# Rotary embedding of the context: from GpSimd to VectorE, in place, in a four-layer decoder kernel

## The chip, the cores and the metric

The kernel runs on one core of a Trainium2 chip. The metric is the time of one execution on the device, in microseconds; before the change the median of three runs is 2383.44 us (2382.97 to 2384.99). The engines are named as in the profile: PE (TensorE, matrix products), DVE (VectorE), ACT (ScalarE), POOL (GpSimd) and SP (SyncE, which here only issues DMA transfers). Each engine works through its own instructions in order and waits for the others by semaphores.

## The reference, cut to what matters

Sixteen sequences of 56 tokens, 256 wide, pass through four layers. Each has an attention on a context of 1500 rows of 64 numbers per sequence and a feed-forward part. Layer 0 attends to the first 56 context rows only (the causal mask leaves no more), and its feed-forward part routes each token to 4 of 16 experts and adds two shared experts. Layers 1 to 3 attend to the whole context, rotated by position:

```python
# layer 0
x = x + jnp.tanh(g_xattn[0]) * _L0_xattn_ref(_layernorm(x), ctx_512, ...)
x = x + jnp.tanh(g_ffn[0]) * _L0_ffn_ref(_layernorm(x), ...)      # 16 experts, top 4, 2 shared
# layer 1 (2 and 3 use the same rotated context)
kv_rope = kv_c * cos[None] + _rotate_half(kv_c) * sin[None]
k_r     = jnp.einsum('bld,hdr->bhlr', kv_rope, W_kr)
scores  = jnp.einsum('bhsr,bhlr->bhsl', q_r, k_r)
ctx_c   = jnp.einsum('bhsl,bld->bhsd', jax.nn.softmax(scores), kv_rope)
```

`_rotate_half(x)` is the second half of the 64 numbers with its sign turned, followed by the first half; the kernel's sine table carries that sign.

## The kernel before, in words

Two sequences make a tile of 112 tokens, so there are 8 tiles (NT). The rotated context of all sequences lies in one buffer, `kv`: 125 partitions, and in each, for each tile, 12 rows of 2 sequences of 64 numbers. It stays in SBUF for the whole kernel. Layer 1 reads it first (L688), when layer 0 is done.

**Layer 0's attention** (`attention_mha`, L380 on) is a pipeline over the 8 tiles (loop at L597): in step i, PE makes the scores of tile i (L509, L515), the transposes of tile i-1 (L540) and its values (L549), and the projection of tile i-2 (L570); DVE takes maxima and differences (L529, L530), ACT the exponentials (L533), and DVE adds the result to the tokens (L573). From step 4 on, the router works through the tiles in four batches of two (`token_tiles`, L1024): DVE normalises the tokens (L1034, L1035; the inverse root by iteration, L131 to L141; L1040), PE transposes (L1048) and multiplies (L1056), DVE takes a softmax and ranks the experts (L1059 to L1074), PE counts places (L1091, L1093), DVE makes the list of slots (L1097 to L1102), and POOL scatters the tokens to their slots in `rows` in DRAM, eight indirect DMAs a batch (L1106). `rows` has been filled with zeros by 16 transfers from SP (`clear_rows`, L1162). All instructions stand in program order on their engines (`in_order`), so a router instruction that waits holds back the attention behind it on DVE and on PE.

**The rotation** (`Roping`, L863) is done on POOL. The context of a tile is loaded to a staging buffer `raw` (two of them, L874) by SP; POOL multiplies it with the cosines into `kv` (L880) and then, for each half, multiplies the other half with the sines (L885) and adds (L886): five instructions a tile. Tiles 0 to 3 are rotated in steps 0 to 3 of the attention; a load waits until POOL has released its staging buffer. Tiles 4 to 7 are rotated during the routed tiles, one part at every second tile; the loads of tiles 6 and 7 are issued just before that loop.

**The routed tiles** (`moe`, L1165; `tiles`, L1283): when the router is done, `table` (L1117) turns the counts into a list of tiles of 128 rows, of which the profiled execution has 34 in layer 0. SP reads the list and loads, three tiles ahead, a tile's expert weights (`wgu` L1197, `wd` L1198) and rows (`xrow` L1204). In tile i, PE multiplies with gate and up weights (L1223), transposes the hidden values of tile i-1 (L1234) and the rows of tile i+1 (L1211), and multiplies tile i-2 with the down weights (L1245); ACT applies the activation (L1227), DVE multiplies (L1228), copies the transposed hidden values (L1236) and makes the list of destinations (L1215); POOL scatters the results (L1248). `during` (L1304) is called at the end of each tile: it places the rotation's parts and, at every fourth tile, a part of the shared experts (L1414, L1425, L1426, L1431, L1433), and from tile 23 on POOL's diagonal matrices (L1318).

Of the kernel before, what the change touches and what calls it, by code (L numbers as in the profile page):

```python
# [36 lines left out]
F32 = mybir.dt.float32  # L37
# [4 lines left out]
ALU = mybir.AluOpType  # L42
# [3 lines left out]
B, S, D = 16, 56, 256  # L46
L, DC = 1500, 64
H = 16
TP = 2 * S
NT = B // 2  # L50
KP, KC = 125, 12
# [14 lines left out]
def bcast(ap, axis, n):  # L66

    ap = ap.unsqueeze(axis)
    shape = list(ap.shape)
    shape[axis] = n  # L70
    return ap.to_broadcast(shape)
# [3 lines left out]
def flamingo_kernel(ctx: ExitStack, tc: tile.TileContext, d: dict, out: bass.AP):  # L75
    nc = tc.nc
# [9 lines left out]
    in_order = tc.keep_in_program_order  # L86
# [20 lines left out]
    kv = const.tile([KP, NT, KC, 2, DC], F32, name="kv")  # L107
# [272 lines left out]
    def attention_mha(router, roping):  # L380
        with ExitStack() as st:
# [10 lines left out]
            def load(name, shape, src, queue):  # L392
                w = ap1.tile(shape, F32, name=name)
                in_order(queue.dma_start(w, src))
                return w


            k0 = ap1.tile([TP, NT, DC], F32, name="k0")

            def load_k0(b, queue):  # L400
                in_order(queue.dma_start(k0[S * b : S * b + S], d["ctx"][:, 0:S, :].rearrange("(t b) s c -> b s t c", b=2)[b]))

            load_x(0, nc.sync)
            load_k0(0, nc.scalar)
# [23 lines left out]
                    in_order(nc.gpsimd.tensor_copy(vbs[i][:, b, :, 32:34], bcast(small[0:TP, C_M : C_M + 2], 1, H // 2)))  # L428
            router.load_weights()
            wo = load("wo", [128, 2, D], d["L0_wo"], nc.gpsimd)  # L430
            for t in range(2):
                roping.load(t, nc.sync)
            clear = clear_rows(ap1)
            for _ in range(6):
                next(clear)
# [2 lines left out]
            for half in range(2):  # L438
# [3 lines left out]
                o = k0d[:, 8 * half : 8 * half + 8]  # L442
                i = bcast(ps[0:DC, 0 : 4 * TP].rearrange("p (n s) -> p n s", s=S), 2, 2)
# [153 lines left out]
            for i in range(NT + 2):  # L597
                new, turn, last = at(i), at(i - 1), at(i - 2)
                if turn:
                    turn.turned()  # L600
                if last:
                    last.turn_context()
                route(i, "a")
                if new:
                    new.scores()
                route(i, "b")
                route(i, "c")
                if new:
                    new.shift()
                    new.exps()  # L610
                route(i, "b")
                if turn:
                    turn.values()
                if last:
                    last.project()
                if turn:
                    turn.normalize()
                if last:
                    last.add()
                if i == 0:  # L620
                    turn_normed(1)
                    queries(1)
                if i + 1 < NT:
                    keys(i + 1)
                    pairs[i + 1].vb = make_values(i + 1)
                route(i, "c")
                route(i, "a")
                route(i, "b")
                route(i, "a")
                route(i, "b")  # L630
                if i < 4:
                    roping.rope(i)
                    roping.load(i + 2, nc.sync)
                    for _ in range(5):
                        next(clear, None)
                if i == 4:
                    load_absorbed(1, 0)
                    load_absorbed(1, 1)
# [223 lines left out]

    class Roping:  # L863
        def __init__(self, pool):
            self.pool, self.raw = pool, {}
            self.cos = pool.tile([KP, KC, DC], F32, name="cos")
            self.sin = pool.tile([KP, KC, DC], F32, name="sin")

        def load(self, t, queue, pool=None):
            if t == 0:  # L870
                in_order(queue.dma_start(self.cos, d["cos_k"]))
                in_order(queue.dma_start(self.sin, d["sin_k"]))
            self.raw[t] = (pool or self.pool).tile([KP, 2, KC, DC], F32, name="raw", bufs=2)
            in_order(queue.dma_start(self.raw[t], d["ctx"][2 * t : 2 * t + 2].rearrange("b (p c) e -> p b c e", c=KC)))  # L874

        def parts(self, t):
            hd = DC // 2
            raw = self.raw.pop(t)
            o = kv[:, t].rearrange("p c b e -> p b c e")
            in_order(nc.gpsimd.tensor_tensor(o, raw, bcast(self.cos, 1, 2), ALU.mult))  # L880
            yield
            for h in range(2):
                mine, other = slice(h * hd, (h + 1) * hd), slice((1 - h) * hd, (2 - h) * hd)
                rot = self.pool.tile([KP, 2, KC, hd], F32, name="rot")
                in_order(nc.gpsimd.tensor_tensor(rot, raw[:, :, :, other], bcast(self.sin[:, :, mine], 1, 2), ALU.mult))  # L885
                in_order(nc.gpsimd.tensor_tensor(o[:, :, :, mine], o[:, :, :, mine], rot, ALU.add))  # L886
                yield

        def rope(self, t):
            for _ in self.parts(t):  # L890
                pass

        def rest(self, st):

            late = st.enter_context(tc.tile_pool(name="rope2", bufs=1, reuse_waits="tile"))
            for t in range(6, NT):
                self.load(t, nc.sync, late)
            for t in range(4, NT):
                yield from self.parts(t)


    class Router:
# [254 lines left out]
    def clear_rows(pool):  # L1157

        zero = pool.tile([128, DX], F32, name="zero")
        in_order(nc.gpsimd.memset(zero, 0.0))  # L1160
        for e in range(16):
            in_order(nc.sync.dma_start(rows[e * CT : (e + 1) * CT].rearrange("c p x -> p c x"), bcast(zero, 1, CT)))  # L1162
            yield

    def moe(r, nxt=None, tail=None, rest=None):  # L1165
# [5 lines left out]
        with ExitStack() as st:  # L1171
# [85 lines left out]
            if l == 0:  # L1257


                sh = Shared(pool, ps_h, ps_o, side)  # L1260
                now = [part for e in range(2) for part in sh.parts(e, 0)]
                between = [part for e in range(2) for part in sh.parts(e, 1)]
                before, last = tail
                next(last)
                now[0][0]()
                next(before)
                next(last)
                next(last)
                next(before)
                next(last)  # L1270
                next(last)
                now[1][0]()
                next(last)
                r.table()
                next(last)
                next(last)
                next(last)
            else:
                r.table()
# [24 lines left out]
            def during(i):  # L1304
                if l == 2 and i == 3:
                    load_absorbed(3, 2)
                if i % 2 == 0 and rest:
                    next(rest, None)
                if i % 4 == 3 and between:
                    for work in between.pop(0):  # L1310
                        work()

                every, ahead = (1, n_sure - 4 - i) if l == 0 else (2, n_sure - 3 - i)
                if ahead >= 0 and ahead % every == 0 and ahead // every < len(by_pe):
                    t = by_pe[len(by_pe) - 1 - ahead // every]
                    diag[t] = pd.tile([TP, top, TP], F32, name=f"diag{t}")
                    for j in range(top):
                        in_order(nc.gpsimd.tensor_scalar(diag[t][:, j, :], ident[0:TP, 0:TP], r.weight[:, t, j : j + 1], None, ALU.mult))  # L1318

            weights, loads = [], []  # L1320
            if l == 0:
                weights = [load_weights(i) for i in range(3)]
                for part in now[0:2]:
                    part[1]()
                for part in now[2:]:
                    for work in part:
                        work()
                r.temporary.close()
                loads = [load_rows(i) for i in range(3)]
                rest = rest(st)  # L1330
                next(rest)
                pd = pool("d", 1)
                r.finish_weights()
            else:
                pd = pool("d", 1)
                r.finish_weights()
                occupy(14 if l == 3 else 8)
                if l == 2:
                    nxt.absorb(0)
# [207 lines left out]
    with tc.tile_pool(name="rope", bufs=1) as rope, routed(0) as r:  # L1547
        roping = Roping(rope)
        tail = attention_mha(r, roping)
        nxt = Next(1)  # L1550
        moe(r, nxt, tail, roping.rest)
    with ExitStack() as keep:
        f1w = keep.enter_context(tc.tile_pool(name="f1w", bufs=1, reuse_waits="tile"))
        matrix = f1w.tile([128, 2, D], F32, name="w8"), f1w.tile([128, 4], F32, name="sc")
# [3 lines left out]
        nxt = Next(2)  # L1558
# [7 lines left out]
    with routed(2) as r:  # L1566
        attention_mla(2, nxt, r)
        nxt.whole.close()
        nxt = Next(3)
# [71 lines left out]
def _arrange(i):  # L1641
    a = {
        "x": i["x"].reshape(B * S, D),
        "ctx": i["ctx_512"],
        "g_xattn": i["g_xattn"].reshape(1, 4),
        "g_ffn": i["g_ffn"].reshape(1, 4),
    }
# [9 lines left out]
    for l in (1, 2, 3):  # L1657
        p = f"L{l}_xattn_"
# [61 lines left out]
```

## Time and profile before

| what | value |
|---|---|
| median of three runs | 2383.44 us |
| profiled execution, its own time | 2402.98 us |
| its span | 2401.2 us |
| granted PE clock, mean | 0.963 |
| layer 0's attention: last addition to the tokens (L573) | 140.65 us |
| first and last routed tile of layer 0 (L1223) | 184.67 and 308.77 us |
| POOL's rotation: 8 L880, 16 L885, 16 L886 | 27.9, 29.5, 29.5 us |
| context loads L874 | 8 of 750 KB |

Times in the table's lower part are from the span's start. The profile gives each engine's busy time and, for the time that an engine sat idle before an instruction, what ended that idle time. Names stand as output<-input; a line is that of the kernel shown. Engine names with a q (SPq) are the instructions that issue DMA transfers: their length is that of the issue, not of the transfer.

### The profile page before, as it was taken

The page shows a single profiled execution, that of the slowest core. Times are in us where ns is not written, and L with a number is a line of the kernel's source. Part 1 is how long each engine was busy: PE and PEld are TensorE (multiplying, and loading weights), DVE is VectorE, ACT ScalarE, POOL GpSimd, SP SyncE. Part 2 cuts the span into 40 slices and gives each one's busy share as a digit, 9 for nine tenths or more (in the row PEclk, how much of TensorE's full clock was granted, in tenths as well). Part 3 has the DMA queues.
Part 4 walks back from the last instruction along what each step waited for, and adds up shares of the span by engine and source line. Part 5 has one row for each costly group of instructions (what it writes and reads, how often), then busy time and mean ns, then how long its engine had stood idle before and what let it go on. Part 6 is the DMA issues. An engine that isn't in the chain of part 4 may idle for free. (4 is left out here: it accounts for less than half of the span.)

```text
span 2401.2 us, 47945 instructions
## 1 busy us (share of the span) xinstructions
PE 2248.3 (94%) x17853; PEld 1613.1 (67%) x17858; DVE 1532.0 (64%) x3546; ACT 1232.0 (51%) x2703; POOL 416.3 (17%) x715
## 2 busy tenths in 40 slices
PE   8668889999999999999999999979899999999697
PEld 5445665777777775447777777745577777777454
DVE  4752245778777777667777777624577777776222
ACT  4312335666666663346666666513566666665131
POOL 5445710000000002420000000001001111101233
PEclk9769999999999999989999999989899999999799
DMA  7726762000000002200000000054101000000596
GB/s 217 225 80 184 215 169 78 22 21 22 21 22 21 21 24 68 61 21 22 23 24 21 13 23 24 10 200 157 32 22 30 29 30 16 28 24 21 153 284 206
DMA packets 116676, 172.98 MB, mean 72 GB/s; under 512 B 20154, under 2 KB 78531, under 8 KB 115412
## 3 DMA queue, kind: packets, MB, share of 16 engines
q1 hardware_dynamic: 106902, 151.35, 20.9%
q0 software_dynamic: 7600, 17.14, 2.2%
q8 instruction: 144, 2.36, 0.4%
q10 hardware_dynamic: 1934, 1.34, 0.2%
q14 instruction: 96, 0.79, 0.1%
HBM read 131.24 MB, written 40.48 MB: 72 GB/s over the span
## 5 line engine op out<-in xcount | busy, mean ns | idle before, releaser
L726 ACT ACTIVATE p<-s_ps,nm 128x500 f32<-128x500 f32 x504 | 335.7, 675 | 364.7 <-DVE nm L717 364.7
L703 PE MATMUL s_ps<-kvT,qT 64*128 64x500 f32 x2016 | 487.5, 610 | 9.9 <-ACT p L735 4.1
L777 PEld LDWEIGHTS m_ps<-pT,kv 125*64 125x64 f32 x8064 | 436.7, 137 | 65.8 <-issue 57.1
L777 PE MATMUL m_ps<-pT,kv 125*64 125x128 f32 x8064 | 477.3, 275 | 1.8 <-ACT pT L770 1.2
L715 DVE TENSOR_REDUCE part<-s_ps 128x1 f32<-128x500 f32 x504 | 340.6, 678 | 216.3 <-PE s_ps L703 215.9
L703 PEld LDWEIGHTS s_ps<-kvT,qT 64*128 64x128 f32 x2016 | 186.7, 190 | 198.1 <-issue 123.8
L765 PE MATMUL m_ps<-ident,p 128*125 128x128 f32 x2016 | 298.3, 283 | 0.4
L720 DVE TENSOR_REDUCE nm<-s_ps 128x1 f32<-128x1500 f32 x168 | 287.2, 1710 | 2.2 <-PE s_ps L703 2.2
L765 PEld LDWEIGHTS m_ps<-ident,p 128*125 128x125 f32 x2016 | 248.2, 188 | 35.9 <-issue 26.1
L735 ACT ACTIVATE p<-s_ps,nm 128x1500 f32<-128x1500 f32 x168 | 254.9, 1517 | 0.8 <-DVE nm L720 0.8
L765 PE MATMUL s_ps<-ident,p 128*125 128x128 f32 x2016 | 249.9, 274 | 0.0
L746 POOL TENSOR_TENSOR den<-den 128x1 f32<-128x1 f32 x168 | 32.9, 196 | 1212.0 <-ACT p L726 1211.8
L765 PEld LDWEIGHTS s_ps<-ident,p 128*125 128x125 f32 x2016 | 234.9, 189 | 0.9 <-ACT p L726 0.2
L770 ACT COPY pT<-s_ps 125x512 f32<-125x512 f32 x336 | 181.0, 596 | 98.5 <-PE s_ps L765 82.8
L770 ACT COPY pT<-m_ps 125x512 f32<-125x512 f32 x336 | 185.3, 617 | 0.2
L1223 PE MATMUL gu_ps<-wgu,xT 128*128 128x448 f32 (+2 forms) x344 | 145.8, 552 | 23.2 <-DMA wgu<-in_L_wgu 14.6
L788 DVE TENSOR_TENSOR ctxT<-m_ps,rep 64x128 f32<-64x128 f32 (+1 forms) x384 | 104.4, 272 | 90.0 <-PE m_ps L777 78.6
L1228 DVE TENSOR_TENSOR act<-gu_ps,act 128x224 f32<-128x224 f32 (+2 forms) x78 | 31.3, 401 | 201.2 <-ACT act L1227 185.2
L768 DVE COPY pT<-m_ps 125x512 f32<-125x512 f32 x168 | 116.2, 692 | 10.0 <-PE s_ps L765 0.9
L312 ACT COPY qT<-q_ps 64x224 f32<-64x224 f32 x128 | 71.8, 561 | 97.2 <-PE q_ps L356 60.4
L1223 PEld LDWEIGHTS gu_ps<-wgu,xT 128*128 128x128 f32 x344 | 64.5, 198 | 76.5 <-issue 35.7
L768 DVE COPY pT<-s_ps 125x512 f32<-125x512 f32 x168 | 114.4, 681 | 0.0
(293 smaller groups left out, 2605.9 us busy)
## 6 DMA issues: line engine op xcount, KB each, us to landing
wgu<-in_L_wgu SPq DMA_DIRECT2D x36, 448.0 KB
rows<-zero SPq DMA_DIRECT2D x16, 899.5 KB
kvT<-turned_kv SPq DMA_DIRECT2D x16, 750.0 KB
wgu<-in_L_wgu SPq DMA_DIRECT2D x34, 352.0 KB
rep<-through SPq DMA_DIRECT2D x336, 32.0 KB
xrow<-rows SPq DMA_DIRECT2D x78, 128.5 KB
wgu<-in_L_wgu SPq DMA_DIRECT2D x8, 1024.0 KB
wd<-in_L_wd SPq DMA_DIRECT2D x36, 224.0 KB
```

Source lines behind the costliest of these rows:

```text
L312: nc.scalar.copy(o, i)
L703: in_order(nc.tensor.matmul(o[:, 0 : 4 * KP], qT[64 * b : 64 * b + 64, t, j * QT : (j + 1) * QT], kvTs[t][64 * b : 64 * b + 64, z * 4 * KP ...
L715: in_order(nc.vector.tensor_reduce(self.part[:, z : z + 1], sp0[z][:, 0 : 4 * KP], AX.X, ALU.max))
L720: in_order(nc.vector.tensor_reduce(self.nm[1], sp1[:, :, 0 : 4 * KP], AX.XY, ALU.max, negate=True))
L726: in_order(nc.scalar.activation(self.p[0][:, 4 * z * KP : 4 * (z + 1) * KP], sp0[z][:, 0 : 4 * KP], AF.Exp, bias=self.nm[0], accum_out=sel ...
L735: in_order(nc.scalar.activation(self.p[1].rearrange("p (z c) -> p z c", z=3), sp1[:, :, 0 : 4 * KP], AF.Exp, bias=self.nm[1], accum_out=se ...
L765: in_order(nc.tensor.transpose(ps[:, c, :], self.p[b][:, k : k + KP], ident))
L768: in_order(nc.vector.tensor_copy(o, ps))
L770: in_order(nc.scalar.copy(o, ps))
L777: in_order(nc.tensor.matmul(self.pv[64 * b : 64 * b + 64, :], kv[:, self.t, c, b, :], self.pT[:, c, b, :], start=c == 0, stop=c == KC - 1))
L788: in_order(nc.vector.tensor_tensor(ctxs[self.t][64 * a : 64 * a + 64, b, lo - 448 * a : hi - 448 * a], self.pv[64 * b : 64 * b + 64, cols] ...
L1223: in_order(nc.tensor.matmul(ps[:, s, 0:n], xT[:, k, :], wgu[:, k, s * n : (s + 1) * n], start=k == 0, stop=k == 1))
```

## The change

- The rotation moves from POOL to DVE and works in place. The context of a tile is loaded straight into its place in `kv`, and only the product with the sines has a buffer of its own, `rot`. A tile takes six DVE instructions of 125 partitions by 768 numbers: two products with the sines, two with the cosines (in two halves of the rows), two additions.
- All 48 are placed in `during`, two at the end of each routed tile, from tile 0 on, until they are used up. The attention has none.
- The loads are eight of one tile each, issued in steps 2 to 5 of the attention behind the clearing of `rows`; the tables of cosines and sines are loaded in step 2. No load of context is left in front of the routed tiles.
- The context comes in another layout from the host, in which a partition's data of a tile lie together; the 56 rows that layer 0 needs come as an array of their own, `keys0`.
- The clearing of `rows` continues after every step until it is through, which takes steps 0 and 1 as before.
- In layer 0, `table` is called two router steps later: behind the last batch's copies and counts of places, in front of its list of slots.

```diff
-                in_order(queue.dma_start(k0[S * b : S * b + S], d["ctx"][:, 0:S, :].rearrange("(t b) s c -> b s t c", b=2)[b]))
+                in_order(queue.dma_start(k0[S * b : S * b + S], d["keys0"][b]))
...
-            for t in range(2):
-                roping.load(t, nc.sync)
             clear = clear_rows(ap1)
...
-                if i < 4:
-                    roping.rope(i)
-                    roping.load(i + 2, nc.sync)
-                    for _ in range(5):
-                        next(clear, None)
+                for _ in range(5):
+                    next(clear, None)
+                if i == 2:
+                    roping.load_tables(nc.sync)
+                if 2 <= i < 6:
+                    roping.load(2 * i - 4, nc.sync)
+                    roping.load(2 * i - 3, nc.sync)
...
+            self.rot = pool.tile([KP, KC, 2, DC], F32, name="rot")
+
+        def load_tables(self, queue):
+            in_order(queue.dma_start(self.cos, d["cos_k"]))
+            in_order(queue.dma_start(self.sin, d["sin_k"]))
+
+        def load(self, t, queue):
+            in_order(queue.dma_start(kv[:, t], d["ctx"][t]))
+
+        def parts(self):
+
             hd = DC // 2
...
+            for t in range(NT):
+                for h in range(2):
+                    mine, other = slice(h * hd, (h + 1) * hd), slice((1 - h) * hd, (2 - h) * hd)
+                    in_order(nc.vector.tensor_tensor(
+                        self.rot[:, :, :, mine], kv[:, t, :, :, other], bcast(self.sin[:, :, mine], 2, 2), ALU.mult
+                    ))
+                    yield
+                for c in (slice(0, KC // 2), slice(KC // 2, KC)):
+                    in_order(nc.vector.tensor_tensor(kv[:, t, c], kv[:, t, c], bcast(self.cos[:, c], 2, 2), ALU.mult))
+                    yield
+                for c in (slice(0, KC // 2), slice(KC // 2, KC)):
+                    in_order(nc.vector.tensor_tensor(kv[:, t, c], kv[:, t, c], self.rot[:, c], ALU.add))
+                    yield
...
                 next(last)
-                r.table()
                 next(last)
                 next(last)
+                r.table()
                 next(last)
...
-                if i % 2 == 0 and rest:
+                if rest:
+                    next(rest, None)
                     next(rest, None)
...
-                rest = rest(st)
-                next(rest)
+                rest = rest()
...
-        "ctx": i["ctx_512"],
+
+        "ctx": i["ctx_512"].reshape(NT, 2, KP, KC, DC).transpose(0, 2, 3, 1, 4),
+        "keys0": i["ctx_512"].reshape(NT, 2, L, DC)[:, :, 0:S].transpose(1, 2, 0, 3),
```

## Prediction

> **What bounds the kernel now.** I read the 40 slices first, then busy time in 10 us windows, then the order of time where PE is not full, then the waits of PE. The slices put layer 0 in the first seventh of the span; layers 1 to 3 (from about 380 us) run at PE 9 in nearly every slice and the change touches none of their instructions, so all that follows is about the first 320 us. Columns of the windows: length; busy time of PE, weight load, DVE, ACT, POOL, each with a count; granted PE clock; DMA share; GB/s.
>
> ```profile
> 50.00:60.00 10.00, 9.95 (x98) 6.78 (x98) 6.27 (x14) 6.71 (x15) 1.05 (x1) 1.00 0.77 247
> 60.00:70.00 10.00, 4.21 (x52) 3.20 (x48) 9.62 (x16) 3.89 (x7) 9.66 (x5) 0.77 1.04 242
> 80.00:90.00 10.00, 5.97 (x42) 3.71 (x41) 9.57 (x8) 5.12 (x10) 9.12 (x4) 0.96 1.04 273
> 90.00:100.00 10.00, 3.88 (x40) 3.62 (x41) 8.80 (x17) 0.95 (x1) 3.22 (x4) 0.50 0.46 149
> 190.00:200.00 10.00, 4.59 (x14) 3.13 (x13) 0.88 (x3) 1.06 (x3) 0.72 (x1) 0.76 0.30 103
> ```
>
> At 50 to 60 PE is full and sets the pace. At 60 to 70 and 80 to 100 PE is half empty while DVE and POOL are both full, and afterwards PE's clock is granted at half. At 190 to 200 everything is empty. The order of time shows DVE and POOL in the first hole (start, length, engine, line):
>
> ```profile
> 62.39 1.86 POOL L885 TENSOR_TENSOR rot<-raw,sin 125x768 f32<-125x768 f32 x1
> 62.94 1.33 DVE L131 TENSOR_SCALAR v<-mv 112x2 f32<-112x2 f32 x1
> 64.31 0.17 DVE L132 TENSOR_SCALAR halfbits<-v 112x2 int32<-112x2 int32 x1
> 64.33 1.81 POOL L886 TENSOR_TENSOR kv<-kv,rot 125x768 f32<-125x768 f32 x1
> 64.52 1.65 DVE L133 TENSOR_SCALAR y<-halfbits 112x2 int32<-112x2 int32 x1
> ...
> 81.27 2.95 DVE L1065 TENSOR_TENSOR p<-p,sum_p 112x32 f32<-112x32 f32 x1
> ...
> 119.99 0.19 DVE L1065 TENSOR_TENSOR p<-p,sum_p 112x32 f32<-112x32 f32 x1
> 120.22 0.69 DVE L1069 TENSOR_TENSOR eq<-p 112x512 f32<-112x512 f32 x1
> ```
>
> A DVE instruction on two elements lasts as long as what is left of POOL's rope beside it (L131 ends 64.27, POOL's L885 64.25). The same L1065 takes 2.95 us beside the rope and 0.19 us at 120, when POOL is idle. PE's waits in 26 to 184 us (total, times, longest) say who pays:
>
> ```profile
> PE m_ps L1048 <- DVE xr L1040: 12.2, 3, 7.3
> PE m_ps L1091 <- DVE sel L1074: 11.2, 2, 8.1
> ```
>
> Both longest waits are in those two holes: the router's DVE chain ends last, stretched by POOL.
>
> **Removed: POOL's rope beside the first router batch.** The chain L131 to the first L1040 takes 62.94 to 70.93 = 7.99 us in batch 0, and 103.41 to 105.78 = 2.37 us in batch 1 with POOL clear: 5.62 us of stretch. The chain L1063 to L1074 takes 80.86 to 93.88 = 13.02 us against 119.58 to 123.59 = 4.01 us: 9.01 us. PE waits behind both, so **-14.6 us**. What is late next: in the first hole PE frees at 64.2 and the unstretched chain gives xr at 65.9, so 1.7 us of waiting stay; in the second sel comes before PE needs it, and PE then waits some 2 us for DVE's L529/L530, as at 97.3 to 99.3 now.
>
> **The clock behind the holes.** After the first hole PE's work of 71.49 to 76.16 took 4.7 us, about 3.1 at full speed (42.4 us has the same matmuls); after the second, L570 takes 2.02 instead of 1.12, and in the next step L449, L458 and L540 take 0.9, 0.9 and 0.8 longer, with a second slow L570. On the path that is 1.5 + 0.9 + 1.8 + 0.9 = 5.1 us, and more if full speed lasts past 115 us. [...] The trace is harsher: 120.7 to 123.8 is a 3.1 us gap and the clock is 0.57 behind it, and it stays at 0.50 from 93 to 108 us although PE is busy 2.7 to 3.0 of 3 us in part of it. Ends 0 and -8; I take **-3**.
>
> **Removed: two context loads in front of the fourth row tile.** Now L874 queues tiles 6 and 7 (750 KB each) on SP just before the fourth xrow:
>
> ```profile
> 179.35 0.99 SPq L874 DMA_DIRECT2D raw<-in_ctx  x2
> 181.09 1.89 SPq L1204 DMA_DIRECT2D xrow<-rows  x1
> 196.23 0.66 PE L1211 MATMUL m_ps<-ident,xrow 128*128 128x128 f32 x2 [5.41 <-DMA xrow<-rows]
> ```
>
> The row tile needs 15 us; PE stands 5.41 us for it, and the routed tile after it takes 198.38 to 205.64 = 7.26 us at a clock of 0.76 and 0.90, where one with the same shared part at full clock takes 214.76 to 220.33 = 5.57. Without those loads on SP there: 5.4 + 1.7 = **-7.1 us** (ends -5 and -8).
>
> **Added: 48 DVE instructions in the tile loop.** Eight tiles of two sequences, six instructions each (2 rot, 2 cos, 2 add), 125x768 f32, two operands in SBUF. No row has that shape on DVE. Near rows: 0.69 us for 112x512 (L1069), 0.34 for 176 elements (L1228): 0.35 us for 336 elements more, so 768 come to 0.69 + 256 x 0.00104 = 0.96 us; POOL's own 1.83 us for it is the upper end. I take 0.96 (both near rows are DVE's): 46 us of DVE, two per tile in tiles 0 to 23. In a tile DVE now does L1228, L1236, L1215 = 0.95 us; with the pair 2.87. A steady tile lasts 2.49 us (L1223 from 236.22 to 238.71) and DVE idles in it mostly here:
>
> ```profile
> 299.55 0.34 DVE L1228 TENSOR_TENSOR act<-gu_ps,act 128x176 f32<-128x176 f32 x1 [1.70 <-ACT act L1227]
> 301.99 1.42 PE L1223 MATMUL gu_ps<-wgu,xT 128*128 128x352 f32 x4 [1.01 <-DMA wgu<-in_L_wgu]
> ```
>
> So the pair (1.91) fills the 1.70 and pushes L1228 late by some 0.4 us per tile. PE asks for that result only after the next tile's four L1223 (1.77 us later), and three tiles in a row add 1.2. Then comes the fourth, with its wait for wgu (1.0 to 1.7) and its shared part (1.9 to 3.2): DVE catches up. The mean tile from 205.64 to 277.48 is 71.84 / 20 = 3.59 us, above 2.87. Hidden therefore; if PE's slack were gone, 24 x 0.38 = 9 us. **+1.5** (0 to 9). Its operands are loaded long before; what stands behind the pair on DVE is the shared parts' L1433 and L1426, whose PSUM buffers PE wants again a tile later. [...] The row: POOL's L1106 beside L1069 to L1072 at 154.6 to 158 take 1.21, 0.94 and 0.93 against a median of 0.94, and L1069 stays at 0.69. I take the row: nothing.
>
> **Moved.** The table goes behind the last batch's four small products on PE (0.53 us each), which start one after another: the table, and with it the first weight loads, come about 1.6 us later, but these (162 us) are used at 184.7. The last slot list, which starts POOL's last eight scatters of 1.24 us, loses its own 1.08 us wait for PE and gains those 1.6, and L1147's product now follows DVE's L1143: **+0.6** (0 to 1.5). Key rows for k0 come as 2 KB instead of 256 B pieces; the x tile behind them (DVE waits 3.76 us for it at 8.6) may land sooner: **-0.5** (-1 to 0). The context loads go past SP's row clearing (16 x 899.5 KB) instead of between it, and SP no longer stops for POOL (at 86.3 it held two loads for 5.8 us). What they delay is the shared weights, which PE needs when attention ends, at 140 now, near 123 then. To be carried by then: 14.7 MB of zeros, 6.1 context, 0.8 tables, 1.9 absorbed weights, 1.1 shared, 2.4 at the start = 27 MB; at the 229 GB/s of 0 to 90 us that is 118 us, at the 198 of 90 to 120 for the rest it is 123. **+1** (0 to 8).
>
> **Sum.** -14.6 - 3 - 7.1 + 1.5 + 0.6 - 0.5 + 1 = -22.1 us. The profiled execution (2402.98 us around a span of 2401.2) would become 2380.9. The median of the runs shown is 2383.44, 19.5 below the profiled one, a cost that I carry over unchanged: **2361 us**.
>
> **Rivals.**
> *Full clock, 0.2.* PE stays warm through the router: -8 instead of -3, nothing for the pair, and some of the slow PE time at 150 to 175 (clock 0.5 to 0.83) goes too, about -2: -31, 2352. For it: the gaps left are short. Against it: the 3.1 us gap above.
> *The transfers bound attention's end, 0.15.* Shared weights land at 131: +8 instead of +1, and the freed clock is lost again (0 instead of -3): -12, 2371. For it: DMA share is 1.04 and more at 60 to 70 and 80 to 90. Against: SP's pauses go.
> *Nothing gained, 0.05.* POOL was not what stretched DVE, or the holes come back behind ACT: only the later loads count, against the pair's 9 us: about 2383.
> *Slower, 0.1.* DVE's rope sets the pace of the routed tiles, held by POOL's scatters. Place: L1228 behind the pair in tiles 0 to 23. With 1.0 us of holding per instruction (2.0 each) a tile costs DVE 4.95, 1.36 above 3.59, x 24 = 33 us, less the 23.6 gained: +9, 2392. It decides from where 0.95 + 2p - 3.59 = 23.6 / 24, p = 1.81 us, just what POOL takes for it. For it: POOL's stretch in attention shows that such holding exists. Against: L1069 and L1106 side by side.
>
> **Chances and range.** The likeliest case has 0.5, its own range 2355 to 2368. Faster by over 0.2% (4.8 us, about what this measurement can tell from none): 0.5 + 0.2 + 0.15 = 0.85; same 0.05; slower 0.10. The range 2348 to 2375 takes in the first three cases and most of their ends.
>
> **What would show it.** Right: L131 to L1040 of batch 0 near 2.4 us, L1063 to L1074 near 4.0; attention's last L573 near 123 us; no wait for xrow at the fourth tile; the rope's instructions near 0.96 us and tile groups of four still near 14 us. Wrong: rope instructions above 1.8 us; PE waiting for L1228's result in each tile; PE waiting for shared weights at attention's end; router chains still stretched.

## The result, and the profile after

The changed kernel takes 2379.82 us (median of 12 runs), the kernel before 2388.66 us (median of 12). The ratio is 0.9966 (95% interval 0.9955 to 0.9976), so about 8 us are gained. (One of the 12 executions of the kernel before took 3187.47 us and is an outlier; the medians hardly feel it.) The forecast was 2361 us, with a range of 2348 to 2375, which the measured time misses by 5 us. The direction was right; the gain is little more than a third of the 22 us that the sum gave.

The holes in the first half of attention are gone. The windows of the profile after (length; busy time of PE, weight load, DVE, ACT, POOL with counts; granted PE clock; DMA share, the mean busy share of the core's 16 DMA engines; GB/s):

```profile
60.00:70.00 10.00, 8.35 (x75) 6.52 (x73) 6.28 (x23) 5.34 (x10) 0.00 (x0) 0.83 0.93 221
70.00:80.00 10.00, 9.98 (x99) 6.81 (x95) 8.45 (x21) 5.20 (x10) 0.00 (x0) 1.00 0.33 120
80.00:90.00 10.00, 7.52 (x56) 5.52 (x54) 7.28 (x28) 3.32 (x7) 0.91 (x1) 0.67 0.31 118
90.00:100.00 10.00, 8.68 (x74) 6.16 (x73) 5.07 (x14) 3.59 (x8) 6.97 (x10) 0.65 0.56 199
...
120.00:130.00 10.00, 1.33 (x4) 0.46 (x2) 7.74 (x29) 1.75 (x3) 4.04 (x7) 0.50 0.89 242
130.00:140.00 10.00, 0.00 (x0) 0.00 (x0) 0.94 (x3) 0.00 (x0) 0.00 (x0) 0.50 0.36 134
```

At 60 to 70 PE is busy for 8.35 us, where it was 4.21; at 90 to 100 for 8.68, where it was 3.88. Then something new comes: from 121 to 143 us PE stands still. The DMA share shows where it begins: from 70 to 90 us it is a third, at 118 to 120 GB/s, although there are context loads waiting to be carried. PE's timeline and its waits in 26 to 200 us (total, times, longest) name what it stood for:

```profile
119.30 2.03 PE L568 MATMUL m_ps<-wo,ctxT 128*112 128x256 f32 x4
142.95 5.81 PE L1406 MATMUL sgu_ps<-xnT,swgu 128*88 128x448 f32 x8 [21.62 <-DMA swgu<-in_L_wgu]
```

```profile
PE sgu_ps L1406 <- DMA swgu<-in_L_wgu: 21.6, 1, 21.6
PE m_ps L1040 <- DVE xr L1032: 8.1, 3, 5.1
...
PE m_ps L1083 <- DVE sel L1066: 3.9, 2, 3.6
```

L568 is the last projection of attention, some 20 us earlier than before. L1406 is the first product with the shared experts' weights, and these have not landed. The waits for the normalised tokens (12.2 before, and 5.2 more that the profile of before puts down to L141) and for the selection (11.2 before) have shrunk. SP's timeline shows what the shared weights stand behind:

```profile
65.14 18.10 SPq L874 DMA_DIRECT2D kv<-in_ctx  x6
83.28 14.48 SPq L231 DMA_DIRECT2D wqr<-in_L_wqr  x1
...
122.89 0.75 SPq L874 DMA_DIRECT2D kv<-in_ctx  x2
124.10 0.35 SPq L1390 DMA_DIRECT2D swgu<-in_L_wgu  x1
```

Six contexts are issued from 65 us on. Behind them SP issues the next layer's weights, and the first of these holds it for 14.48 us; among SP's waits from 65 to 126 us, 10.6 us are for contexts to land. So SP comes to the last two contexts only at 122.9 and to the shared weights at 124.1 (before: 113.2), and these take another 19 us to land.

The router's chains on DVE, the rotation on DVE, and POOL's scatters in the tile loop, each from its own view (start, length, engine, line; then for the rotation minimum, median and maximum in ns):

```profile
63.05 0.16 DVE L131 TENSOR_SCALAR v<-mv 112x2 f32<-112x2 f32 x1
65.41 0.73 DVE L1032 TENSOR_SCALAR xr<-x,mv,y 112x256 f32<-112x256 f32 x2
...
75.46 0.19 DVE L1057 TENSOR_TENSOR p<-p,sum_p 112x32 f32<-112x32 f32 x1
```

```profile
L882 DVE TENSOR_TENSOR rot<-kv,sin x16: 941/948/951, 187.4 to 258.3; 125x768 f32<-125x768 f32 x16
```

```profile
193.14 1.89 POOL L1240 DMA_INDIRECT results<-y,to  x1 [17.67 <-ACT y L1239]
195.63 1.82 POOL L1240 DMA_INDIRECT results<-y,to  x1 [0.60 <-ACT y L1239]
```

L131, which took 1.33 us beside POOL's rotation, takes 0.16; L1057 takes 0.19, where it took 2.95. The rotation takes 0.948 us. The scatters, 0.97 to 1.04 us before, take up to 1.89 beside it.

### The profile page after: what moved, and what is told of

It reads as the page before. It is cut to its first block, busy times and chain, and to the rows that moved or that the text cites. A ratio compares the mean times of both kernels' runs of the same rounds, so it can differ in the third digit from the quotient of the medians.

```text
span 2379.4 us, 47898 instructions
## 1 busy us (share of the span) xinstructions
PE 2231.1 (94%) x17853; PEld 1602.9 (67%) x17858; DVE 1557.5 (65%) x3594; ACT 1230.4 (52%) x2703; POOL 342.0 (14%) x675
## 3 DMA queue, kind: packets, MB, share of 16 engines
q8 instruction: 144, 2.36, 0.4%
## 5 line engine op out<-in xcount | busy, mean ns | idle before, releaser
L1215 PE MATMUL gu_ps<-wgu,xT 128*128 128x448 f32 (+2 forms) x344 | 139.6, 532 | 22.9 <-DMA wgu<-in_L_wgu 16.0
L1240 POOL DMA_INDIRECT results<-y,to x78 | 91.1, 1167 | 198.3 <-ACT y L1239 190.6
```

The costliest lines, as they stand in the source:

```text
L1215: in_order(nc.tensor.matmul(ps[:, s, 0:n], xT[:, k, :], wgu[:, k, s * n : (s + 1) * n], start=k == 0, stop=k == 1))
L1240: i = nc.gpsimd.indirect_dma_start(flat, bass.IndirectOffsetOnAxis(ap=to[:, 0:1], axis=0), y, None, bounds_check=B * S * top - 1, oob_is_e ...
```

## The experiments

**First question: is it the amount to be carried, or how it is carried?** 0.33 and 0.31 are close to 5/16, as if five of the 16 engines carried a load. A context load has 125 partitions, and 5 is the largest number up to 16 that divides 125. That the two belong together is a guess so far, from these numbers alone. The first experiment cuts each load in 112 partitions, which 16 divides, and 13.

```diff
-            in_order(queue.dma_start(kv[:, t], d["ctx"][t]))
+            in_order(queue.dma_start(kv[0:112, t], d["ctx"][t, 0:112]))
+            in_order(queue.dma_start(kv[112:KP, t], d["ctx"][t, 112:KP]))
```

> The changed kernel, with each context load cut in two: 112 partitions and 13. Theory A (a load of 125 partitions is carried by 5 of the 16 DMA engines, 5/16 = 0.31, the DMA share of 70 to 90 us; the shared weights stand behind contexts on those five): the DMA share of 65 to 90 us rises to 0.8 or more, the contexts are through some 25 us earlier, PE's wait of 21.6 us for the shared weights falls under 4 us, and the time falls by 15 to 22 us against the changed kernel, to about 2361 (ratio to before about 0.989). Rival B (the amount carried, or the chain of transfers that each wait for the one eight back, sets the time): share and wait stay (wait above 15 us), time 2377 to 2382.

Measured: 2362.96 us, ratio to before 0.9892 (0.9877 to 0.9906). Its windows and PE's timeline:

```profile
70.00:80.00 10.00, 9.80 (x111) 7.38 (x110) 8.95 (x25) 6.19 (x12) 0.00 (x0) 1.00 0.94 219
80.00:90.00 10.00, 6.38 (x37) 4.40 (x34) 7.17 (x29) 3.88 (x7) 1.96 (x2) 0.56 0.80 211
```

```profile
117.75 2.03 PE L568 MATMUL m_ps<-wo,ctxT 128*112 128x256 f32 x4
119.57 4.50 PE L1407 MATMUL sgu_ps<-xnT,swgu 128*88 128x448 f32 x8
```

The DMA share goes from 0.33 and 0.31 to 0.94 and 0.80. The last two contexts and the shared weights are issued at 100.2 and 102.1 us instead of 122.9 and 124.1, and PE goes from its last projection (117.75) to the first shared product (119.57) without a wait. Bytes and order are the same; only the pieces differ. Theory A holds, in share, wait and time.

The opposite cut, 64 and 61 partitions (the same two lines with 64 for 112; no number from 2 to 16 divides 61), tells whether it matters how the partitions divide, or whether any two pieces are better than one:

> The changed kernel, with each context load cut in two pieces of 64 and 61 partitions. Theory A (a load goes to as many engines as the largest number up to 16 that divides its partitions; 61 has none but 1): each piece of 61 (366 KB) goes through one engine at 120/5 = 24 GB/s, 15.6 us each and 125 us for eight, the shared weights wait behind them, PE's wait for them grows from 21.6 us to 50 us or more, and the time is above 2405 us. Rival B (any cut in two loads the engines more evenly): as with 112 and 13, wait under 4 us, time near 2363.

PE's timeline, then SP's:

```profile
213.22 3.29 PE L1407 MATMUL sgu_ps<-xnT,swgu 128*88 128x448 f32 x4 [89.56 <-DMA swgu<-in_L_wgu]
```

```profile
71.29 15.26 SPq L874 DMA_DIRECT2D kv<-in_ctx  x1
...
88.01 15.91 SPq L874 DMA_DIRECT2D kv<-in_ctx  x1
```

The one execution took 2450.14 us, 56 above the median of the kernel before beside it, with PE waiting 89.6 us. Four of the pieces of 64 hold SP for 15.3 to 16.2 us each, about what the expectation gave for a piece of 61 on one engine (15.6 us). From 100 to 120 us the DMA share is 0.23 and 0.15, at 61 and 52 GB/s. So cutting alone gains nothing; where the cut lies decides.

The traces also keep the start and length of each DMA packet, so the packets under way at a time can be counted. Whole loads have five packets under way for 88% of the time from 72 to 90 us, and six for the rest. With 112 and 13 there are 13 to 17 for 84% of the time from 70 to 80 us; with 64 and 61 there is one for 91% of the time from 110 to 118 us. The largest numbers up to 16 that divide 125, 112 and 61 are 5, 16 and 1, so the counts agree with theory A of both experiments. Two loads of the changed kernel's routed tiles (160 to 310 us) fit as well: those of 88 partitions (`wd`; 11 divides 88) have more than 11 packets under way for 4% of their time, those of 128 (`wgu`; 16 divides 128) for 44%. For other numbers nothing is shown here.

**Does the order do as well?** Here the tables and contexts go behind the shared weights, whole as they were:

```diff
-                if i == 2:
-                    roping.load_tables(nc.sync)
-                if 2 <= i < 6:
-                    roping.load(2 * i - 4, nc.sync)
-                    roping.load(2 * i - 3, nc.sync)
...
                 sh = Shared(pool, ps_h, ps_o, side)
+                rest.__self__.load_tables(nc.sync)
+                for t in range(NT):
+                    rest.__self__.load(t, nc.sync)
```

> The changed kernel, with the tables of cosines and sines and all eight context loads issued behind the shared weights instead of in front of them; the loads themselves are unchanged. Theory A (only the order before the shared weights matters, slow contexts elsewhere are hidden): the 21.6 us wait goes, attention still ends near 121 us, the contexts run at a DMA share near 0.3 until about 155 us, and the time is near 2361. Rival B (slow contexts then hold back the first routed tiles' weights or rows): the wait goes, but the first routed tile comes no earlier than 178 us, and the time stays above 2370.

Measured: 2371.12 us, ratio 0.9936 (0.9922 to 0.9950). The time is rival B's, the first routed tile (174.46 us) comes earlier than B said. The 21.6 us wait is gone, but the ratio falls by only 0.30 points from the changed kernel's 0.9966, where the split brought 0.74. From SP's timeline and PE's waits in 26 to 330 us:

```profile
102.05 35.75 SPq L869 DMA_DIRECT2D kv<-in_ctx  x8
```

```profile
PE sy_ps L1421 <- DVE shT L1416: 7.1, 2, 6.4
PE m_ps L1198 <- DMA xrow<-rows: 4.4, 2, 4.1
```

SP needs 35.75 us to issue the eight loads, and the work behind them comes late: PE waits 4.1 us for the first rows, and the first routed tile starts 52.0 us behind the first shared product, against 43.4 with the split loads. Here too, narrow loads go with delay in what is queued behind them; the order alone does not cure it.

**What does the rotation on DVE cost?** Left out, in one line (`rest = None` for `rest = rest()`):

> The changed kernel with the 48 rotation instructions on DVE left out (layers 1 to 3 attend to unrotated context; layer 0 computes the same, and is what is compared). Theory A (the rotation is hidden in the tile loop): first to last gate-and-up product of layer 0 takes 110 to 111.5 us, as with it (111.5), and layer 1's first scores come within 1.5 us of 375.9. Rival B (it costs its time on DVE): the loop takes 103 to 106 us.

The routed tiles of layer 0 take 112.27 us from the first to the last product with gate and up, against 111.47 with the rotation. That is 0.8 us over theory A's bracket and far from rival B's 103 to 106, and in seven further profiles with the rotation on DVE the loop takes 110.26 to 115.04 us: no cost of the rotation shows. Layer 1's first scores come at 371.79 instead of 375.92, which theory A had not allowed, but the loop began 4.9 us earlier. (The whole takes 2416.62 us, because unrotated context sends the tokens of the later layers to more tiles, 84 in all instead of 78; this says nothing of the rotation's cost.) POOL's scatters show what the rotation does to them:

```profile
188.20 1.01 POOL L1240 DMA_INDIRECT results<-y,to  x1 [18.14 <-ACT y L1239]
190.69 0.99 POOL L1240 DMA_INDIRECT results<-y,to  x1 [1.48 <-ACT y L1239]
```

0.97 to 1.03 us without the rotation, mostly 1.77 with it: POOL is held for 0.8 us by DVE. No cost shows in the loop; POOL waits for ACT in front of 23 of the 32 scatters up to 300 us anyway.

**Is the stretch of the router's chains POOL's doing?** On the kernel with split loads, dummy work of the rotation's size on POOL:

```diff
+        def beside(self, t):
+            r = self.rot.rearrange("p c b e -> p (c b e)")
+            in_order(nc.gpsimd.tensor_tensor(r[0:TP, 0:D], x[:, t, :], r[0:TP, 0:D], ALU.mult))
+            in_order(nc.gpsimd.tensor_tensor(r, r, r, ALU.mult))
+            for k in (0, 1, 0, 1):
+                o = r[:, 768 * k : 768 * k + 768]
+                in_order(nc.gpsimd.tensor_tensor(o, o, o, ALU.mult))
...
                 if last:
                     last.add()
+                if i in (4, 5):
+                    roping.beside(i - 2)
```

> The changed kernel with context loads of 112 and 13 partitions, and with dummy work on POOL: behind the additions for tiles 2 and 3 in attention, each time six multiplications of zeros in the rotation's buffer (one small, one of 125x1536, four of 125x768 numbers), as much as POOL's rotation of a tile before. Their results are not used. Theory A (POOL's two-input work beside DVE's stretches the router's chains): PE's waits for the normalised tokens and for the selection grow to 6 us and more each, attention's last product comes at 130 to 138 us instead of 117.75, and the time is 12 to 18 us above that of the kernel with the split loads, near 2376. Rival B (the stretch came from the transfers or from SP's waits for POOL): attention's last product comes within 3 us of 117.75, time near 2364.

Measured: 2384.16 us, ratio 0.9964 (0.9948 to 0.9980), 0.72 points above the kernel with split loads, or 17 us, and 16 us above the kernel with split loads that ran on the same chip (2368.17 us, below). From the timelines of POOL and of DVE:

```profile
65.57 5.74 POOL L879 TENSOR_TENSOR rot<-rot 125x768 f32<-125x768 f32 x4
```

```profile
67.08 1.39 DVE L140 TENSOR_TENSOR v<-v 112x2 f32<-112x2 f32 x1
68.51 1.39 DVE L141 SCALAR_TENSOR_TENSOR y<-v,y 112x2 f32<-112x2 f32 x1
69.93 1.39 DVE L139 TENSOR_TENSOR v<-y 112x2 f32<-112x2 f32 x1
71.36 0.18 DVE L140 TENSOR_TENSOR v<-v 112x2 f32<-112x2 f32 x1
```

Each DVE instruction on two elements a partition takes as long as one of POOL's (5.74 / 4 = 1.4 us), and falls back to 0.18 when POOL is through, at 71.3. PE's wait for the normalised tokens grows to 9.3 us at the longest; the one for the selection only to 4.9, short of the 6 expected. Attention's last projection comes at 137.35, against 117.75 and, on the same chip, 123.59. That work on POOL stretches the router's chains and delays attention is shown.

**What do narrow loads do in the kernel before?** The same cut there, on `raw`:

```diff
+            src = d["ctx"][2 * t : 2 * t + 2].rearrange("b (p c) e -> p b c e", c=KC)
+            in_order(queue.dma_start(self.raw[t][0:112], src[0:112]))
+            in_order(queue.dma_start(self.raw[t][112:KP], src[112:KP]))
```

> The kernel before, with each of its context loads cut in 112 and 13 partitions. Theory A (the fourth row tile stood behind two contexts on five engines): PE's wait of 5.4 to 5.9 us for it falls under 1.5 us and the slow tile behind it goes, attention ends within 2 us of where it did, and the time falls by 5 to 9 us, ratio 0.997. Rival B (the bytes in front of it hold it, whatever the engines): the wait stays above 4 us, ratio 0.999 to 1.001.

Measured: 2374.15 us, ratio 0.9921 (0.9903 to 0.9939). The row tile's part (PE's wait for the fourth `xrow`) came as expected, but the gain is over twice the 5 to 9 us expected, and attention's end was missed: the last projection came at 125.94 us, 8.7 to 12.7 us earlier than in the two profiles of the kernel before. POOL's timeline in the kernel before, then POOL's, DVE's, and PE's waits in this kernel say why:

```profile
58.95 3.52 POOL L880 TENSOR_TENSOR kv<-raw,cos 125x1536 f32<-125x1536 f32 x1 [10.70 <-DMA raw<-in_ctx]
```

```profile
47.96 3.54 POOL L882 TENSOR_TENSOR kv<-raw,cos 125x1536 f32<-125x1536 f32 x1 [1.92 <-DMA raw<-in_ctx]
...
57.12 1.81 POOL L888 TENSOR_TENSOR kv<-kv,rot 125x768 f32<-125x768 f32 x1
```

```profile
63.51 0.16 DVE L131 TENSOR_SCALAR v<-mv 112x2 f32<-112x2 f32 x1
...
65.87 0.73 DVE L1042 TENSOR_SCALAR xr<-x,mv,y 112x256 f32<-112x256 f32 x2
```

```profile
PE m_ps L1213 <- DMA xrow<-rows: 2.0, 6, 0.7
```

In the kernel before, POOL began tile 2 at 58.95 us, after waiting 10.70 us for its context, and was in it while the router's first chain ran. With the context in time, tile 2 is rotated from 48 to 59 us, before the chain starts at 63.5, and the chain is not stretched. Tile 3 is through at 78.0 us, and the second chain takes 5.9 us instead of 13.0. Most of the collision that the change removes was itself a consequence of the narrow loads, and so was the stall at the fourth row tile: PE's longest wait for rows falls from 5.4 us to 0.7.

**The table's place**, on the kernel with split loads, put back to where it was:

> The changed kernel with context loads of 112 and 13 partitions, and with the table of layer 0 called where it was before, one router step behind the last batch's selection. Theory A (the move of the table is worth little): within 3 us of the kernel with the split loads, 2360 to 2366, ratio to before 0.988 to 0.991. Rival B (it brings the first weights later and costs 3 us or more): 2360 or less, first routed tile 3 us or more earlier behind the first shared product than 43.4 us.

2368.17 us, ratio 0.9899 (0.9883 to 0.9916), inside theory A by the ratio though not by the time, on another chip. From the first shared product to the first routed tile it takes 43.90 us, against 43.36 with the table moved: no cost of the move shows.

**The kernel before once more**, for a second profile:

> The kernel before, unchanged, for a second profile. Theory A (its first profiled execution, 2402.98 us, lost about 14 us in layers 2 and 3 that are not there in most executions): the span is 2383 to 2390, layer 0 takes as long as before (first routed tile near 184.7, layer 1's first scores near 386.7), and layer 3's first scores come near 1689 instead of 1701. Rival B (the profile adds its time everywhere, or in layer 0): layer 1's first scores come 8 us or more earlier than 386.7.

The profiled execution took 2384.33 us, against 2402.98 of the first. Layer 1's first scores come at 378.96 (first profile 386.73), layer 3's at 1688.90 (1701.16), layer 3's last routed tile at 2350.12 (2369.46). Neither theory is right alone: of the 19 us, 8 lie in layer 0, where attention ends 4 us earlier, and 11 are spread over code that the change does not touch. The medians do not have them: they belong to that one execution.

**Four corners on one chip**, then the tables cut as well (`cos` and `sin`, also 125 partitions):

> The changed kernel itself, once more, so that the four corners (before or changed, context loads whole or split) stand on one chip. Theory A (the change's gain is taken back by the five-engine loads): ratio to before 0.995 to 0.998, wait for the shared weights 18 us or more. Rival B (the small gain belonged to one chip): ratio 0.990 or less, or 1.0 or more.

> The kernel before with context loads of 112 and 13 partitions, once more. Theory A (in the kernel before, too, the contexts' late arrival put POOL's rotation beside the router's chains; with them in time POOL is through with tile 2 before the first chain): ratio 0.991 to 0.994, the rotation of tile 2 ends before 62 us, the first chain is not stretched. Rival B (an outlier): ratio above 0.996.

> The changed kernel with context loads of 112 and 13 partitions, once more. Theory A (with the loads on all engines the move of the rotation still wins what is left of the stretch, attention's end at 118 against 126): 3 to 10 us below the kernel before with the split loads, ratio to before 0.987 to 0.991. Rival B (with the loads split, the move is worth nothing): within 2 us of it.

> As the kernel of the last run, and the tables of cosines and sines cut in the same way. Theory A (nothing waits for the transfers any more once the contexts are split): within 2 us of it, no wait for the shared weights. Rival B (the tables' 750 KB on five engines still delay the shared weights): 3 us or more below it.

| kernel | median us | ratio to before | interval |
|---|---|---|---|
| before | 2386.86 | 1 | |
| changed | 2375.12 | 0.9958 | 0.9942 to 0.9974 |
| before, loads split | 2365.85 | 0.9913 | 0.9890 to 0.9935 |
| changed, loads split | 2362.18 | 0.9902 | 0.9881 to 0.9923 |
| changed, loads and tables split | 2359.98 | 0.9896 | 0.9872 to 0.9919 |

The changed kernel's ratio came as theory A had it, with a wait for the shared weights of 17.3 us (18 or more was expected). In the kernel before with split loads the rotation of tile 2 ends at 59.3 us and the first chain is not stretched, as expected. The split gains more in the kernel before than the move of the rotation does: the intervals 0.9890 to 0.9935 and 0.9942 to 0.9974 lie apart.

With the loads split the move of the rotation is worth 3.7 us by the medians, but the intervals overlap: a small gain is likely (on other chips the same two kernels stood at 0.9921 and 0.9892), and not shown by these runs. At attention's end there is next to nothing left to win: the last projection comes at 119.53 us with the rotation on DVE and at 120.99 with it on POOL (118 against 126 was expected), while the same attention with the rotation on DVE ended anywhere from 117.75 to 123.59 us in profiles on other chips. The tables' cut is not told apart from none. The version with both cuts has the lowest median here, 27 us or 1.1% below before.

## Why the prediction was right and wrong

**Right: the stretch.** Measured as in the forecast, from start to start, L131 to the first L1032 takes 63.05 to 65.41 = 2.36 us (2.4 was forecast), the chain to the selection 75.05 to 79.07 = 4.02 (4.0). The last addition of attention comes at 121.4 us (123 was forecast).

**Wrong: "at the 229 GB/s of 0 to 90 us that is 118 us" (+1, 0 to 8).** This step failed, and it decides the miss. In its place PE waited 21.6 us for the shared weights in one profile of the changed kernel and 17.3 in another. The mechanism stood among the rivals as "the transfers bound attention's end", at 0.15 and +8. The 27 MB were about right (28.9 MB moved up to 143 us); the rate was not. 229 GB/s was the mean of a time in which context loads mostly ran beside clearing transfers (DMA share 0.88 from 30 to 60 us and 0.94 from 60 to 90). The change puts all the contexts behind the clearing, alone, and alone they get 118 to 120 GB/s at a share of 0.31 to 0.33. From 65 to 143 us the mean was 160 GB/s. The argument against this rival, "SP's pauses go", failed with it: SP no longer waits for POOL, but it is held behind the contexts and issues the shared weights 11 us later than before. The profile of before gave a sign, had the DMA share been read beside the GB/s; both windows (the second stands in the prediction) have context loads in flight:

```profile
20.00:30.00 10.00, 9.00 (x42) 4.50 (x41) 3.72 (x8) 3.16 (x7) 3.56 (x2) 1.00 0.41 149
```

A share of 0.41 and 0.46 left the engines more than half idle, and from 20 to 30 us five packets were under way for 74% of the time, though clearing transfers stood in SP's queue.

**Wrong: "a cost that I carry over unchanged" (19.5 us).** The profiled execution was not the kernel plus a fixed cost of profiling. The second profile of before took 2384.33 us, and the profiled execution after lies 1.6 us above its own median. The forecast of the median does not rest on this cost, since 2383.44 - 22.1 gives it as well. But that my 2380.9 us for the profiled execution meets the measured 2381.4 is an accident: 20 us of transfers were missed, and some 19 us that only the first execution had lost were counted in.

**Right in direction, too small: the fourth row tile.** The wait for it is gone (0.2 us are left). The tile loop falls from 124.10 us in the first profile and 120.05 in the second to 111.47 (layer 0, first to last product). -7.1 + 1.5 was forecast, -8.6 to -12.6 measured. What it was put down to, two loads in front, was incomplete: cut in 112 and 13, the same loads in the same place leave 0.7 us of waiting.

**Right: the rotation's cost and cover.** 0.948 us against 0.96; no cost for the loop shows, where +1.5 was taken.

**Wrong without consequence: "I take the row: nothing".** From a row of L1069 beside L1106 the forecast took it that POOL's scatters and DVE's rotation would leave each other alone. In the tile loop the scatters went from 0.97 to 1.77 us. They were held by DVE, not DVE by them (the rotation's instructions stay at 0.941 to 0.951 us), and no cost for the loop shows, so the slower rival did not come. No run shows the 1.0 us of holding per DVE instruction that this rival reckons with.

**The small terms.** For the table +0.6 was taken, and -0.5 measured in single profiles. DVE's longest wait for an x tile went from 3.76 to 2.70 us; -0.5 was taken for the keys. The clock's -3 cannot be read apart from attention's end: with the stretch and the keys -18.1 was forecast, and -19.3 (first profile) and -15.3 (second) measured. At 60 to 70 us 0.83 was granted, where it was 0.77; at 80 to 100 us 0.67 and 0.65, where it was 0.96 and 0.50. How long a gap of PE the full clock outlasts was not shown: at 60 to 70 us, with PE busy for 8.35 and 8.34 us, 0.83 was granted in the changed kernel and 1.00 with the loads cut in 64 and 61. The 0.57 that the forecast read behind the 3.1 us gap is the mean of 123 to 126 us, which takes in the end of the gap; from 123.8 us on 0.50 was granted.

Between the second profile of before and the profile after the books are: attention -15.3 us, from its end to the first routed tile +20.3, the tile loop -8.6, the rest of layer 0 +0.5, together -3.0; a single profile scatters by a few us around the 8 that the medians give.

## What to carry to other kernels

Read the DMA share beside the GB/s: here a plateau at a third, while transfers were waiting, was a transfer with five packets under way, and the rate averaged over mixed traffic (229 GB/s) did not say what that transfer got alone (118 to 120). Before an engine is relieved of work, ask why the work stood where it collided; here late data had put it there, and three lines on the loads were worth more than moving the rotation. A single profile can lie far from the median of its kernel (here 14 to 20 us, by the median taken); compare the sum with a second profile before its difference is carried along.

## What the runs showed of the hardware

- A load of 125 partitions ran at a DMA share of 0.31 to 0.33 and 118 to 120 GB/s, with five packets under way; cut in 112 and 13, at 0.80 to 0.94 and 211 to 219; cut in 64 and 61, at 0.15 to 0.23 and 52 to 61, with one packet under way for 91% of 110 to 118 us.
- The shared weights, issued 1.2 us behind two whole contexts, landed 19 us after their issue, and PE waited 21.6 us; with the contexts cut in 112 and 13 they were issued 22 us earlier, and PE did not wait.
- The holding of DVE and POOL goes both ways: DVE's two-element instructions took 1.39 us beside POOL's of 1.4 us, and POOL's scatters took 1.77 instead of 0.97 us beside DVE's rotation, whose own length stayed at 0.941 to 0.951 us.
